# Four-layer graph network, one core: comparing a tile of ranks with itself in one operation, the diagonals of r on GpSimd, and the short tile's row sum on VectorE

## The chip, the cores and the metric

The kernel runs on 1 core of one Trainium2 chip. A core has a matrix engine (TensorE, PE in the profile; its weight loads are shown as PEld), a vector engine (VectorE, DVE), an activation engine (ScalarE, ACT), GpSimd (POOL) and a queue engine (SyncE, SP). Each engine works through its own instructions in order, and waits on semaphores for the others. SP, ACT and POOL issue transfers (DMA) between the chip's memory (HBM) and the on-chip memory (SBUF); TensorE writes to a separate accumulator memory (PSUM), which is read out by VectorE or ScalarE.

The metric is device microseconds (us) of one execution. The kernel before took 853.08 us, the median of 4 runs (850.79, 852.27, 853.89 and 853.95).

## The reference, cut to what matters

Four layers work on `x` (2708 nodes by 128 features) and on `adj` (2708 by 2708, zeros and ones with ones on the diagonal). Each starts with a layer norm and a relu and adds its result to `x`. The change lies in the last layer:

```python
XW = h @ W
s_col = XW @ a[0, :f]
s_row = XW @ a[0, f:]
Z1 = leaky_relu(s_row[:, None] + s_col[None, :], negative_slope=0.01)
den = exp(Z1)
num = A @ den
att = where(num != 0, den / num, 0)
x = x + A @ (att @ XW)
```

Below, `r` is `s_row` and `c` is `s_col`, one number per node. Since `den[i, j]` is `exp(r_i + c_j)` where the sum is positive and `exp(0.01 (r_i + c_j))` where it is not, `A @ den` can be built from sums over nodes sorted by `r`. So the kernel needs the rank of every node in `r`.

## The kernel before

The 2708 nodes lie in T = 22 tiles of 128 rows; the last holds 20 rows (`rows(t)`). They are also grouped into six blocks of 512 columns (`TILES[b]`, `E0[b]`). The scheduler of the tile framework decides the order of instructions on each engine, except where a line asks for program order. The work of layer 4 goes through these stages:

1. **Making r.** For each block b the loop that ends at L727 takes the previous layer's result, transposes it, adds it to `xs`, makes the layer norm (`bn_stats` L184, `bn_aggr` L185, `isq` L172 on VectorE; a power function for `rstd` L173 on GpSimd; `shift` L189 on VectorE; the relu L191 on ScalarE), transposes again, copies to `hT` (L705, ScalarE) and multiplies by the weights (L209). The products are copied out in groups of three tiles, c = 0, 3, ..., 21 (`hs`, L210, VectorE). Column P+1 of them is r; L712 and L713 put it into `r_of`, with nodes beyond 2708 moved far away. Each group's r is then needed along the free dimension of all partitions: VectorE multiplies the identity by r (`diag`, L717), TensorE multiplies a matrix of ones by that (L724, into the one buffer `acc4`), and ScalarE copies the result to `row_b` (L727). `diag` has two buffers.
2. **Ranks.** `row_b` now has all r along the free dimension, `r_of[:, t]` has tile t's along the partitions. For tiles in groups of three (c), four VectorE operations on 128x384 elements compare a tile with itself: `own` (L735, greater), `tie` (L736, greater or equal), `tie` times the strict triangle `before` (L737), and the maximum of both (L738); `own` and `tie` have one buffer each. For each tile t, VectorE then compares all earlier tiles with it (`bits`, L744, 128 by 128t; two buffers), ScalarE sums `bits` along the row into `rowsum` (L747, with `row_a` as a place for the copy it makes), and TensorE sums `bits` and `own` down the columns (L753, L757) into one accumulator.
3. **From ranks to tables.** L761 copies the accumulator, four transposes (L764) turn it, `below` (L766) takes the row sums off, L782 makes a second copy of r in `row_a`, and L770 to L776 give `rank`. A long row of small VectorE operations follows (from `ge`, L673), with TensorE matmuls between; it orders nodes by c as well.
4. **Sums.** `sums(t)` loads tile t of the transposed adjacency (L828, SP's queue) and adds it up with weights that depend on the rank (L835). The loads of the first tiles wait in SBUF during stages 1 and 2; the others start as buffers come free.
5. **Densities.** `densities(s0)` does the same trick of diagonal (L1088), matmul (L1095), scale (L1102, L1104), L1105 and exponential (L1106) for four slots at a time. The first three calls (s0 = 0, 4, 8; `FIRST = 3`) stand between the last `sums`, the other eight after them.
6. **Main loop.** GpSimd gathers rows of the adjacency and of the prefix sums by index (L647), and for 22 steps TensorE forms `num` (L1206), ScalarE and VectorE form the attention, and TensorE adds it up (L1150). A last product with the adjacency gives the result.

Of the kernel before, what the change touches and what calls it, by code (L numbers as in the profile page):

```python
# [8 lines left out]
F32 = mybir.dt.float32  # L9
BF16 = mybir.dt.bfloat16  # L10
# [9 lines left out]
def kernel(  # L20
# [436 lines left out]
    nc.vector.memset(ones_b, 1.0)  # L457
    before = const.tile([P, P], BF16, name="before")
    nc.vector.tensor_scalar(before, lane, part, None, ALU.is_gt)
    first = const.tile([P, P], F32, name="first")  # L460
    nc.vector.memset(first, 0.0)
    nc.vector.memset(first[0:1, :], 1.0)
# [23 lines left out]
    def rest(exact, stack3):  # L486
# [182 lines left out]
        with tc.tile_pool(name="tab", bufs=1) as tab, tc.tile_pool(name="tabs", bufs=2) as tabs:  # L669
# [17 lines left out]
            for b in range(NB):  # L687
                lo, hi = E0[b]
                n = len(TILES[b])
                ts = slice(TILES[b][0], TILES[b][-1] + 1)  # L690
                nc.scalar.activation(yT[:, lo:hi], row_b[:, lo:hi], AF.Relu, bias=tot[:, 6:7], scale=tot[:, 5:6])
                p = acc_bank(b % 2)
                turned(p, yT, TILES[b], True)
                f = len([t for t in TILES[b] if t < TF])
                nc.vector.tensor_add(
                    xs[:, ts.start : ts.start + f, :].rearrange("p t d -> p (t d)"),
                    xs[:, ts.start : ts.start + f, :].rearrange("p t d -> p (t d)"),
                    p[:, : f * P],
                )
                if f < n:  # L700
                    nc.vector.tensor_add(xs[:TAIL, TF, :], xs[:TAIL, TF, :], p[:TAIL, cols(f)])
                layernorm(b, hn)
                p = acc_bank(2 + b % 2)
                turned(p, hn, TILES[b])
                nc.scalar.copy(hT[:, spans(b)], p[:, : n * P])  # L705
                t0 = done
                while done < T and min(done + 3, T) <= ts.stop:
                    project(w3_ext, done, bank())
                    done += 3

                new = slice(t0, min(done, T))
                nc.vector.tensor_mul(r_of[:, new], r_col[:, new], valid[:, new])  # L712
                nc.vector.tensor_add(r_of[:, new], r_of[:, new], far[:, new])  # L713
                for c in range(new.start, new.stop, 3):
                    m = min(3, new.stop - c)
                    diag = tabs.tile([P, 4, P], F32, tag="diag", name="diag")
                    nc.vector.tensor_tensor(  # L717
                        diag[:, :m],
                        ident[:, None, :].to_broadcast([P, m, P]),
                        r_of[:, c : c + m, None].to_broadcast([P, m, P]),  # L720
                        ALU.mult,
                    )
                    p = acc_bank(4)
                    nc.tensor.matmul(  # L724
                        p[:, : m * P], ones, diag[:, :m].rearrange("p t q -> p (t q)"), start=True, stop=True
                    )
                    nc.scalar.copy(row_b[:, c * P : (c + m) * P], p[:, : m * P])  # L727
            nc.scalar.dma_start(xw_d.rearrange("(t p) d -> p t d", p=P), hs[:, :, :P])
            for c in range(0, T, 3):
                m = min(3, T - c)  # L730
                own = tabs.tile([P, 3, P], BF16, tag="own", name="own", bufs=1)
                tie = tabs.tile([P, 3, P], BF16, tag="tie", name="tie", bufs=1)
                mine = row_b[:, c * P : (c + m) * P].rearrange("p (t q) -> p t q", q=P)
                theirs = r_of[:, c : c + m, None].to_broadcast([P, m, P])
                nc.vector.tensor_tensor(own[:, :m], mine, theirs, ALU.is_gt)  # L735
                nc.vector.tensor_tensor(tie[:, :m], mine, theirs, ALU.is_ge)  # L736
                nc.vector.tensor_mul(tie[:, :m], tie[:, :m], before[:, None, :].to_broadcast([P, m, P]))  # L737
                nc.vector.tensor_max(own[:, :m], own[:, :m], tie[:, :m])  # L738
                for q in range(m):
                    t = c + q  # L740
                    r = rows(t)
                    if t:
                        bits = tabs.tile([P, N], BF16, tag="bits", name="bits")
                        nc.vector.tensor_scalar(  # L744
                            bits[:r, : t * P], row_b[:r, : t * P], r_of[:r, t : t + 1], None, ALU.is_gt
                        )
                        nc.scalar.activation(  # L747
                            row_a[:r, : t * P], bits[:r, : t * P], AF.Identity, accum_out=rowsum[:r, t : t + 1]
                        )
                        for k in range(NB):  # L750
                            x0, x1 = E0[k][0], min(E0[k][1], t * P)
                            if x1 > x0:
                                nc.tensor.matmul(  # L753
                                    rk[:NB, : x1 - x0], pick_b[:r, k, :], bits[:r, x0:x1], start=False, stop=False
                                )
# [328 lines left out]
            def densities(s0):  # L1084
                n = min(4, NS - s0)
                diag = tabs.tile([P, 4, P], F32, tag="diag", name="diag")
                z = dmat[:, s0 : s0 + n, :]
                nc.vector.tensor_tensor(  # L1088
                    diag[:, :n],
                    ident[:, None, :].to_broadcast([P, n, P]),  # L1090
                    c_two[:, s0 : s0 + n, None].to_broadcast([P, n, P]),
# [236 lines left out]
```

## Time and profile before

| | |
|---|---|
| median of 4 runs | 853.08 us (850.79 to 853.95) |
| time of the profiled execution | 852.42 us |
| its span, first to last instruction | 850.6 us |
| PE / DVE / ACT / POOL busy | 730.5 / 583.4 / 536.4 / 190.1 us |
| stage 1 (making r), in the span | about 382 to 410 us |
| stage 2 (ranks), in the span | about 399 to 442 us |
| stage 3 and the loads of stage 4 | 442 to 506 us |
| stage 5, the last eight calls, to the start of the main loop | 506 to 534 us |

Times in the profile are microseconds from the start of the span. A timeline line has start, duration, engine, source line, operation, output<-inputs, shapes and, in brackets, how long the engine had been idle before it and what ended that. A group line has the count, the busy time in us and the mean duration in ns, and after the bar the idle time before them. The chain of work is read from the end backwards: each piece is what released the next, or what stood before it on its engine. ("issue" in it is time with no visible cause.) One row by window has the busy time and count of PE, PEld, DVE, ACT and POOL, then TensorE's granted clock as a share of full speed, the share of the DMA engines and GB/s.

### The profile page before, as it was taken

To read this page: it belongs to the slowest core of one execution; us is meant where nothing else is said; L and a number is where in the kernel's file an instruction comes from. 1 tells how busy PE (TensorE), PEld (TensorE's weight loads), DVE (VectorE), ACT (ScalarE), POOL (GpSimd) and SP (SyncE) were. 2 spreads that over 40 slices of the span, in tenths; PEclk is the share of its full clock that TensorE was granted. 3 is DMA by queue.
4 is the path that set the end of the run, shared out by engine and by line. 5 is a ranking of instruction groups with operands and counts; after the bars stand their busy time and mean duration, and the time that the engine had idled before them with its cause. 6 is when DMAs were issued, how large, how long until landed. Compare 5 with 4: busy or idle time off the path is not lost.

```text
span 850.6 us, 9005 instructions
## 1 busy us (share of the span) xinstructions
PE 730.5 (86%) x3113; PEld 440.6 (52%) x3113; DVE 583.4 (69%) x1112; ACT 536.4 (63%) x595; POOL 190.1 (22%) x161
## 2 busy tenths in 40 slices
PE   3599999995996979978759785799999999989996
PEld 2333333342775858755226531555555555545785
DVE  5499879886834363447988967776666666655854
ACT  3889999995845574537770025687777787767000
POOL 3000000012201010002000122346666667620010
PEclk9899999997897989988679995799999999999999
DMA  9044445723997989975504985677777777785994
GB/s 336 6 145 183 173 164 186 304 80 137 358 400 267 364 341 403 418 300 200 195 0 154 399 342 212 240 290 262 267 261 280 276 270 264 281 307 227 417 428 144
DMA packets 39475, 218.63 MB, mean 257 GB/s; under 512 B 5107, under 2 KB 13998, under 8 KB 25358
## 3 DMA queue, kind: packets, MB, share of 16 engines
q1 hardware_dynamic: 27704, 150.19, 45.8%
q0 software_dynamic: 8624, 65.76, 21.3%
q10 hardware_dynamic: 3090, 1.99, 0.7%
q8 instruction: 27, 0.44, 0.2%
q14 instruction: 30, 0.25, 0.1%
HBM read 214.12 MB, written 3.79 MB: 256 GB/s over the span
## 4 chain that ended last, share of the span: by engine, by line
PE 13%; DMA 12%; DVE 10%; issue 7%; POOL 6%; ACT 4%; SPq 0%; DVEq 0%; POOLq 0%; ACTq 0%
DMA hs<-in_adj_t_dram 4%; PE bank L1206 4%; PE acc L1150 3%; DMA row_b<-pre_d,pre_i 2%; DMA yT<-pre_d,pre_i 2%; POOL hs L647 2%; PE acc L224 2%; DMA row_b<-in_adj_t_dram 2%; ACT rows L1168 2%; POOL hT L647 2%; DVE bits L744 1%; POOL yT L647 1%; DVE rows L1283 1%; POOL row_b L647 1%; PE acc L835 1%
## 5 line engine op out<-in xcount | busy, mean ns | idle before, releaser
L1206 PE MATMUL bank<-rows,d_hi 128*128 128x512 f32 (+1 forms) x264 | 106.4, 407 | 24.0 <-ACT ln L1211 12.3
L224 PE MATMUL acc<-rows,h_hi 128*128 128x512 f32 (+1 forms) x264 | 106.2, 407 | 11.0 <-ACT rows L529 6.5
L1150 PE MATMUL acc<-e,xw 128*128 128x512 f32 (+1 forms) x264 | 104.3, 545 | 0.0
L1211 ACT ACTIVATE ln<-bank,tiny 128x512 f32<-128x512 f32 x132 | 79.8, 633 | 33.1 <-PE bank L1206 33.1
L1206 PE MATMUL bank<-rows,d_lo 128*128 128x512 f32 (+1 forms) x264 | 98.5, 384 | 0.0
L224 PE MATMUL acc<-rows,h_lo 128*128 128x512 f32 (+1 forms) x264 | 98.0, 387 | 0.2 <-DVE h_lo L506 0.2
L1214 DVE TENSOR_TENSOR e<-e,ln 128x1536 f32<-128x1536 f32 (+2 forms) x66 | 69.7, 1095 | 15.3 <-ACT ln L1211 15.0
L1206 PEld LDWEIGHTS bank<-rows,d_hi 128*128 128x128 f32 x264 | 51.4, 195 | 52.7 <-ACT ln L1211 29.7
L358 DVE SCALAR_TENSOR_TENSOR tau<-tau,e_hi,a 128x1536 f32<-128x1536 f32 (+1 forms) x44 | 70.5, 1623 | 10.0 <-ACT tau L355 3.9
L1150 PEld LDWEIGHTS acc<-e,xw 128*128 128x128 f32 x264 | 48.4, 190 | 52.6 <-issue 52.6
L355 ACT ACTIVATE tau<-row_a,e_neg,e_lo 128x1536 f32<-128x1536 f32 (+1 forms) x44 | 66.0, 1510 | 3.5 <-PE bank L367 3.3
L224 PEld LDWEIGHTS acc<-rows,h_hi 128*128 128x128 f32 x264 | 52.4, 199 | 24.9 <-ACT rows L529 8.6
L367 PE MATMUL bank<-tau,ones_at 128*32 128x512 f32 (+1 forms) x264 | 51.8, 566 | 8.3 <-DVE tau L358 8.3
L224 PEld LDWEIGHTS acc<-rows,h_lo 128*128 128x128 f32 x264 | 52.4, 199 | 11.7 <-issue 1.9
L1220 ACT ACTIVATE e<-e 128x2708 f32<-128x2708 f32 x22 | 54.2, 2461 | 3.6 <-DVE e L1214 3.6
L224 PE MATMUL acc<-yT,hs 128*128 128x512 f32 x132 | 56.3, 564 | 0.0
L224 PE MATMUL acc<-row_b,hs 128*128 128x512 f32 x132 | 55.3, 557 | 0.0
L1206 PEld LDWEIGHTS bank<-rows,d_lo 128*128 128x128 f32 x264 | 51.5, 195 | 7.0
L224 PE MATMUL acc<-rows,y_hi 128*128 128x512 f32 x132 | 49.1, 379 | 4.4 <-DVE rows L1283 2.5
L224 PE MATMUL acc<-rows,y_lo 128*128 128x512 f32 x132 | 47.7, 376 | 0.0
L1189 DVE TENSOR_SCALAR xw<-xw,c_exp 128x128 f32<-128x128 f32 x22 | 6.3, 285 | 58.7 <-DMA xw<-xw_d,xw_i 58.7
L529 ACT CAST rows<-dflat 128x1536 fp32r<-128x1536 f32 (+1 forms) x26 | 34.2, 1331 | 18.9 <-DMA dflat<-in_adj_dram 10.3
(411 smaller groups left out, 1419.7 us busy)
## 6 DMA issues: line engine op xcount, KB each, us to landing
a<-in_adj_dram SPq DMA_DIRECT2D x21, 1354.0 KB
rows<-in_adj_t_dram SPq DMA_DIRECT2D x16, 1354.0 KB
dflat<-in_adj_t_dram SPq DMA_DIRECT2D x9, 768.0 KB
rows<-in_adj_t_dram SPq DMA_DIRECT2D x9, 768.0 KB
dflat<-in_adj_dram SPq DMA_DIRECT2D x9, 768.0 KB
rows<-in_adj_dram SPq DMA_DIRECT2D x9, 768.0 KB
dflat<-in_adj_t_dram SPq DMA_DIRECT2D x5, 1354.0 KB
hs<-in_adj_t_dram SPq DMA_DIRECT2D x5, 1354.0 KB
```

The lines of the kernel that those rows point to most:

```text
L224: nc.tensor.matmul(accs[b][:, : hi - lo], w, moving[:, lo - at : hi - at], start=start and i == 0, stop=stop and i == len(parts) - 1,)
L355: nc.scalar.activation(tau[:, :w], row_a[:, h0:h1], AF.Relu, bias=e_neg[:, t : t + 1], scale=e_lo[:, t : t + 1])
L358: nc.vector.scalar_tensor_tensor(tau[:, :w], tau[:, :w], e_hi[:, t : t + 1], a[:, h0:h1], ALU.add, ALU.mult)
L367: nc.tensor.matmul(den[g : g + 32, : hi - lo], ones_at[:, b // GR, :], tau[:, lo - h0 : hi - h0], start=(t == 0 and b < GR), stop=(t == T ...
L529: m = nc.vector.tensor_copy(r, a) if i % 2 and i > 4 else nc.scalar.copy(r, a)
L647: return nc.gpsimd.indirect_dma_start(out=out, out_offset=None, in_=src, in_offset=bass.IndirectOffsetOnAxis(ap=idx, axis=0),)
L1150: m = nc.tensor.matmul(accs[b][:, : hi - lo], xw, e[:, lo:hi], start=(s == 0), stop=(s == NE - 1))
L1168: m = nc.scalar.copy(r, a) if q % 2 else nc.vector.tensor_copy(r, a)
L1206: m = nc.tensor.matmul(num[:, : hi - lo], d, a[:, lo:hi], start=(i == 0), stop=(i == len(products) - 1))
L1211: nc.scalar.activation(ln[:, lo:hi], num[:, : hi - lo], AF.Ln, bias=tiny)
L1214: tc.keep_in_program_order(nc.vector.tensor_sub(e[:, beg:hi], e[:, beg:hi], ln[:, beg:hi]))
L1220: tc.keep_in_program_order(nc.scalar.activation(e, e, AF.Exp))
```

## The change

- A constant `tie_at` is made once, before the layers: minus 2 to the power of -126 in the strict triangle, zero elsewhere.
- Each tile is compared with itself by one VectorE operation on 128x128: `(row_b - r_of) > tie_at`, three of them for a group of three tiles, in place of the four operations on 128x384. `own` takes the pool's two buffers; `tie` goes.
- The diagonals of r (L717) are made by GpSimd.
- The row sum of the last tile (20 rows by 2688) is a VectorE reduction in place of the ScalarE pass.
- The diagonals of the first three calls of `densities` (s0 below 12) are made by GpSimd.

```diff
+    tie_at = const.tile([P, P], F32, name="tie_at")
+    nc.vector.tensor_scalar_mul(tie_at, before, -(2.0**-126))
...
                     diag = tabs.tile([P, 4, P], F32, tag="diag", name="diag")
-                    nc.vector.tensor_tensor(
+                    nc.gpsimd.tensor_tensor(
                         diag[:, :m],
...
-                own = tabs.tile([P, 3, P], BF16, tag="own", name="own", bufs=1)
-                tie = tabs.tile([P, 3, P], BF16, tag="tie", name="tie", bufs=1)
-                mine = row_b[:, c * P : (c + m) * P].rearrange("p (t q) -> p t q", q=P)
-                theirs = r_of[:, c : c + m, None].to_broadcast([P, m, P])
-                nc.vector.tensor_tensor(own[:, :m], mine, theirs, ALU.is_gt)
-                nc.vector.tensor_tensor(tie[:, :m], mine, theirs, ALU.is_ge)
-                nc.vector.tensor_mul(tie[:, :m], tie[:, :m], before[:, None, :].to_broadcast([P, m, P]))
-                nc.vector.tensor_max(own[:, :m], own[:, :m], tie[:, :m])
+                own = tabs.tile([P, 3, P], BF16, tag="own", name="own")
+                for q in range(m):
+                    t = c + q
+                    nc.vector.scalar_tensor_tensor(
+                        own[:, q, :], row_b[:, cols(t)], r_of[:, t : t + 1], tie_at, ALU.subtract, ALU.is_gt
+                    )
...
-                        nc.scalar.activation(
-                            row_a[:r, : t * P], bits[:r, : t * P], AF.Identity, accum_out=rowsum[:r, t : t + 1]
-                        )
+                        if t == T - 1:
+                            nc.vector.tensor_reduce(rowsum[:r, t : t + 1], bits[:r, : t * P], AX.X, ALU.add)
+                        else:
+                            nc.scalar.activation(
+                                row_a[:r, : t * P], bits[:r, : t * P], AF.Identity, accum_out=rowsum[:r, t : t + 1]
+                            )
...
                 z = dmat[:, s0 : s0 + n, :]
-                nc.vector.tensor_tensor(
+                (nc.gpsimd if s0 < 4 * FIRST else nc.vector).tensor_tensor(
                     diag[:, :n],
```

## The prediction

> **What bounds the kernel now.** I read the page, then the windows, to see which engine fills the stage that the change touches, then the chain of work there, then the timelines of VectorE and ScalarE. Everything that is edited lies in 382 to 442 us, but for three diagonals at 493 to 498 us and one constant.
>
> ```profile
> 397.00:410.00 13.00, 10.44 (x47) 6.01 (x48) 12.36 (x51) 7.25 (x22) 0.84 (x1) 0.91 0.54 180
> 410.00:442.00 32.00, 21.73 (x83) 8.15 (x82) 27.61 (x53) 29.28 (x38) 0.00 (x0) 0.71 0.22 73
> ```
>
> From 397 to 410 VectorE is full (12.36 of 13 us) and GpSimd idle. From 410 to 442 VectorE (27.61 of 32) and ScalarE (29.28) are both nearly full. The chain of waits goes through both:
>
> ```profile
> 410.42 0.20 ACT row_a L747
> ...
> 410.64 0.62 DVE bits L744
> 411.27 0.46 DVE own L735
> ...
> 438.08 2.54 ACT row_a L747 x2
> ...
> 440.65 0.18 DVE below L766
> ...
> 442.23 0.17 DVE rank L770
> ```
>
> ScalarE's timeline shows when its row sums start and where they halt:
>
> ```profile
> 408.36 0.48 ACT L727 COPY row_b<-acc 128x384 f32<-128x384 f32 x1 [3.09 <-PE acc L724]
> ...
> 413.55 1.06 ACT L747 ACTIVATE row_a<-bits 128x1024 f32<-128x1024 bf16 x1
> ...
> 416.48 1.27 ACT L747 ACTIVATE row_a<-bits 128x1280 f32<-128x1280 bf16 x1 [0.49 <-DVE bits L744]
> ...
> 421.38 1.59 ACT L747 ACTIVATE row_a<-bits 128x1664 f32<-128x1664 bf16 x1 [0.43 <-DVE bits L744]
> ...
> 433.26 2.23 ACT L747 ACTIVATE row_a<-bits 128x2432 f32<-128x2432 bf16 x1
> ```
>
> So the sums wait 3.09 us for the copies of r; later ScalarE sets the pace but for 0.92 us in which VectorE is late. I cut at two points: A, from 390.35 (the first diagonal) to the sum of tile 8 (413.55); B, from there to the sum of tile 19 (433.26); C, from there to `rank` (442.23). What follows (VectorE's table operations without a pause to 485, then loads at 0.87 to 0.99 of the DMA engines to 504, then gathers) waits for `rank` or for buffers freed after it, so a shift of `rank` should reach the end whole.
>
> **Prices.**
>
> ```profile
> L735 DVE TENSOR_TENSOR own<-row_b,r_of 128x384 bf16<-128x384 f32 x7 | 3.9, 550 | 0.5 <-PE acc L757 0.5
> ...
> L737 DVE TENSOR_TENSOR tie<-tie,before 128x384 bf16<-128x384 bf16 x7 | 2.4, 348 | 0.0
> ...
> L1105 DVE SCALAR_TENSOR_TENSOR dflat<-dflat,flatter 128x512 f32<-128x512 f32 x11 | 8.2, 747 | 3.0 <-ACT dflat L1102 3.0
> ...
> L339 DVE TENSOR_REDUCE deg<-a 128x1 f32<-128x2708 f32 x2 | 5.9, 2964 | 0.0
> ...
> masks.py:199 POOL TENSOR_SCALAR_AFFINE_SELECT ident<-ident 128x128 f32<-128x128 f32 x1 | 0.3, 293 | 0.0
> ...
> L75 POOL MEMSET hn<- 128x1172 f32 x1 | 1.7, 1704 | 35.0 <-DVE rows L529 35.0
> ...
> L75 POOL MEMSET row_b<- 128x1172 f32 x1 | 1.1, 1077 | 5.0 <-DVE rows L529 5.0
> ```
>
> - *Own comparison.* Starts of consecutive VectorE instructions lie 0.08 us closer than their durations, so four old operations hold VectorE 2 x 0.47 + 2 x 0.27 = 1.48 us per group. The new one is L1105 at 128 instead of 512 elements: two-input rows grow 1.05 ns per element (L1088's 512 against L717's 384: 682 - 542 ns), so 0.747 - 0.40 = 0.35; L735 at 128x128 took 0.29, the low end. I take 0.30 and 0.22 of VectorE's line: 0.66 per group, 0.8 saved seven times.
> - *Diagonal on GpSimd, 128x384.* No row shows a GpSimd multiply. L173 is a power function, not near. The select took 0.293 for 128 elements, one read and one write; memsets (0.205 at 128, 2.36 at 2708) give a fixed 0.1, so 1.5 ns per element for two streams, 2.25 for three: 0.1 + 384 x 2.25 ns = 0.97 us, which I take. Low end: VectorE's 0.55. High end: the memset of `hn` beside VectorE's copies took 1.58 times its twin: 1.53 us.
> - *Reduction, 20x2688 bf16.* L339 scaled: 2.94 us, taken as the nearest row. Low end: half, 1.5, since L737 on 16-bit data takes 0.35 where L735 takes 0.55.
>
> A weighing: the Trainium skill, "GPSIMD Engine Reference", section 3.1, has a two-input elementwise operation of 2048 elements at 4497 ns on GpSimd against 2293 on VectorE, and says VectorE stays the rule. My estimate from it is 0.84 us for 384 elements, by which the sum below would be 0.3 us better.
>
> **A.** I stepped the new order of each engine with the durations of these rows and of the timeline. (The old order, stepped alike, gives 413.28 for the sum of tile 8 where the trace has 413.55, so I compare stepped with stepped.) VectorE's line loses 8 diagonals (7 x 0.47 + 0.2 = 3.5 us) and, up to tile 8, 3 x 1.48 us of old comparisons; it gains 12 x 0.22 and ten small operations on `r_exp` and `r_low`, 0.8 us, that ran later: 4.5 us less. Not all of it is gain. A chain takes its place: diagonal 0.97, matmul 0.75, copy 0.48 us per group, through one PSUM buffer, with three L209 products now standing behind the first diagonal's matmul on TensorE, so the copy of group c=3 moves from 395.08 to 396.2 and that of c=15 from 404.8 to 405.7. GpSimd's queue hides only the next `rstd`, which the first diagonal ends in time for (390.85 against 392.29). The one DMA in ScalarE's queue there (`xw_d`, L728) stays at its place, 405.2 against 405.34; SP's queue is not passed. But ScalarE no longer has the copies of c=18 and 21 ahead of the sums of tiles 4 to 6: tile 4 starts at 406.1 (409.89 before). Then VectorE is late again: it does six own comparisons (1.3) and eleven small ones (1.2) before the bits of tile 6, so tile 6 comes at 409.8 (411.50) and tile 8 at 412.3. A = 412.3 - 413.3 = -1.0. With 0.55 us per diagonal it is -2.0, with 1.53 it is +1.3.
>
> **B.** ScalarE's durations for tiles 8 to 18 sum to 17.50 us, plus 11 x 0.12 between starts: 18.8, against 19.7. VectorE has slack now (bits of tiles 8 to 20 plus ten comparisons are under 16 us), and `own` no longer waits for TensorE with two buffers: -0.9. Ends: -0.9, and 0 if the halts stay.
>
> **C.** The bits of tile 21 wait for the sum of 19 (2.36 after its start), take 1.61, the reduction 2.94; then L761, which now stands behind it (0.60), `below` (0.10) and L782 (1.48): 9.06 with gaps, against 8.97. +0.1. ScalarE's pass of 2.44 goes, but something of equal length takes its place. With a reduction of 1.5 TensorE's column sums of tile 21 are next (439.69 in the trace): -0.4.
>
> **Nothing for the rest.** The constant (0.2 us) falls into VectorE's 0.54 us wait at 15 us. The three diagonals at 493 us: 128x512 by the same row is 1.25 us from 492.9; TensorE comes to the first at 495.2, behind sums that wait for loads. If that cover went, 0.6 us. The gather behind them on GpSimd's queue starts at 503, after loads; the third diagonal is over near 497.6.
>
> Sum: -1.0 - 0.9 + 0.1 = -1.8: the profiled execution's 852.42 becomes 850.6 (span 848.8). It was 0.66 under the median; on the median's scale 853.08 - 1.8 = **851.3 us**.
>
> **Does GpSimd hold up VectorE?** Two-input VectorE operations inside a GpSimd instruction ran at normal length (L712 at 399.71 in 0.15 us, inside the `rstd` of 399.50, and the pair below), though that instruction reads only four elements per partition:
>
> ```profile
> 392.36 0.15 DVE L713 TENSOR_TENSOR r_of<-r_of,far 128x3 f32<-128x3 f32 x1
> 392.29 1.01 POOL L173 TENSOR_TENSOR rstd<-isq,neg_half 128x4 f32<-128x4 f32 x1 [3.57 <-DVE r_of L712]
> ```
>
> The Trainium skill's page "SBUF — State Buffer", section "SBUF: two separate sides", says the pair of SBUF ports shared by VectorE and GpSimd is an exclusive lock, for VectorE operations with two SBUF inputs or two ports. Stepped with such a lock, tile 8 comes at 413.2 and the sum is -0.9 instead of -1.8.
>
> **Rivals.**
> 1. *GpSimd becomes the bound (slower).* One mechanism: six diagonals in a row (c=3 to 18) carry r to ScalarE, each on the chain. Above 1 us every 0.1 us per diagonal costs 0.4. The point of no gain is 1.4 us. At 2.0 us A is +3.5, the sum +2.7: 855.8. For it: 1.53 by the contended memset, and VectorE is at 12.36 of 13 us there. Against: 0.97 by the select.
> 2. *More gain.* Diagonals at 0.55, comparisons at 0.21 per operation, the short reduction: A -2.4, B -0.9, C -0.4 = -3.7: 849.4. For it: VectorE's waits for TensorE at a clock of 0.71 shrink. Against: nothing shows GpSimd level with VectorE.
> 3. *No change.* The load of `row_b` at 489.06 takes 15.03 us behind others; if the loads are held by bandwidth and not by `rank`, the shift is eaten: 853.1. Against: no byte moves from 420 to 442, so loads start only after `rank`.
>
> **Chances and range.** About 0.3% (2.6 us) is what a measurement of this kernel can tell from no change. Forecast 0.48 (its own range 849.5 to 853, four tenths of it past 0.3%), more gain 0.21, slower 0.20, no change 0.11. Faster 0.19 + 0.21 = 0.40, same 0.29 + 0.11 = 0.40, slower 0.20. The range runs from 1 us of run scatter below rival 2, 848.4, to rival 1 at 2.0 us, 855.6.
>
> **What would show it.** Right: POOL diag rows near 1 us; the sum of tile 4 near 406 and of tile 8 near 412, no halt from there; `rank` near 440.4; the reduction near 2.9 us. Wrong: POOL diag rows above 1.4 us, VectorE rows stretched beside them, or `rank` early and the loads' end at 504 not.

## The result, and the profile after

| | before | after |
|---|---|---|
| median of all runs | 853.1 us (70 runs, 847.56 to 859.31) | 853.48 us (44 runs, 849.22 to 858.91) |
| ratio after / before, 95% interval | | 1.0011 [1.0000, 1.0021] |
| profiled execution, its span | 852.42, 850.6 us | 855.91, 854.1 us |
| first r_of (L712, after: L715) | 389.44 | 390.07 |
| from there to the sum of tile 8 | 24.11 | 25.28 |
| sum of tile 8 to sum of tile 19 | 19.71 | 19.15 |
| sum of tile 19 to `rank` | 8.97 | 9.03 |
| first r_of to `rank` | 52.79 | 53.46 |
| `rank` to the landing of the load into `row_b` | 61.90 | 64.58 |

By the ratio the kernel became slower by 0.1%, 0.9 us, where 1.8 us less was forecast. (The medians of all runs lie only 0.4 us apart, and the interval begins at no change; the forecast gain lies outside it.) The stage begins 0.63 us later in the profile of after than in that of before, ahead of everything in the stage that was changed; in all the profiles below the first r_of lies anywhere from 388.96 to 391.71 us. So all stages are counted from the first r_of. (Lines of after are 3 or 4 higher than before's: L720 is the diagonal, L730 the copy to `row_b`, L737 the own comparison, L745 `bits`, L749 and L751 the row sums, L774 `rank`, L839 the sums.)

The two windows of the stage, after:

```profile
397.00:410.00 13.00, 10.28 (x48) 6.37 (x47) 8.90 (x28) 8.36 (x26) 4.93 (x7) 0.87 0.55 195
410.00:443.00 33.00, 19.27 (x84) 7.82 (x84) 28.05 (x57) 25.61 (x33) 0.34 (x1) 0.88 0.22 73
```

VectorE, which was full (12.36 of 13 us) from 397 to 410, now counts 8.90 us, and GpSimd 4.93 instead of 0.84. Yet the stage is no shorter. ScalarE's timeline shows where it halts:

```profile
407.95 0.48 ACT L730 COPY row_b<-acc 128x384 f32<-128x384 f32 x1 [1.36 <-PE acc L727]
408.33 0.63 ACT L751 ACTIVATE row_a<-bits 128x512 f32<-128x512 bf16 x1
...
413.05 0.84 ACT L751 ACTIVATE row_a<-bits 128x768 f32<-128x768 bf16 x1 [3.01 <-DVE r_exp_p L793]
...
415.35 1.06 ACT L751 ACTIVATE row_a<-bits 128x1024 f32<-128x1024 bf16 x1
```

Tile 4 does start earlier (18.26 us after the first r_of; 20.45 before), but then ScalarE waits 3.01 us for VectorE, and tile 8 is 1.17 us late. VectorE's timeline has two reasons. Rows that take longer than elsewhere show when GpSimd's timeline is laid beside it, and brackets show waits for TensorE:

```profile
391.24 0.38 DVE L172 TENSOR_SCALAR isq<-mv 128x4 f32<-128x4 f32 x1
...
394.48 0.73 DVE L172 TENSOR_SCALAR isq<-mv 128x4 f32<-128x4 f32 x1
...
399.64 2.03 DVE L737 SCALAR_TENSOR_TENSOR own<-row_b,r_of,tie_at 128x128 bf16<-128x128 f32 x3
...
405.02 0.56 DVE L210 COPY hs<-bank 128x390 f32<-128x390 f32 x1 [2.28 <-PE bank L209]
...
408.34 0.55 DVE L745 TENSOR_SCALAR bits<-row_b,r_of 128x640 bf16<-128x640 f32 x1 [0.78 <-PE acc L757]
...
408.88 2.40 DVE L737 SCALAR_TENSOR_TENSOR own<-row_b,r_of,tie_at 128x128 bf16<-128x128 f32 x6
```

```profile
390.77 0.83 POOL L720 TENSOR_TENSOR diag<-ident,r_of 128x384 f32<-128x384 f32 x1 [1.43 <-PE acc L198]
...
394.37 0.83 POOL L720 TENSOR_TENSOR diag<-ident,r_of 128x384 f32<-128x384 f32 x1 [1.66 <-DVE r_of L716]
...
399.86 1.66 POOL L720 TENSOR_TENSOR diag<-ident,r_of 128x384 f32<-128x384 f32 x2 [1.68 <-DVE r_of L716]
...
409.11 1.23 POOL L720 TENSOR_TENSOR diag<-ident,r_of 128x384 f32<-128x384 f32 x2 [2.16 <-DVE r_of L716]
```

For comparison, two of these operations on VectorE with no GpSimd multiply beside them (own_only, below):

```profile
391.55 0.16 DVE L172 TENSOR_SCALAR isq<-mv 128x4 f32<-128x4 f32 x1
...
405.53 0.86 DVE L737 SCALAR_TENSOR_TENSOR own<-row_b,r_of,tie_at 128x128 bf16<-128x128 f32 x3
```

An `isq` on four elements per partition takes 0.16 us there; the one that begins at 394.48 ends at 395.21, with the diagonal (394.37 + 0.83 = 395.20). The one at 391.24 ends at 391.62, the diagonal at 391.60. Three own comparisons that take 0.86 us undisturbed take 2.03, six take 2.40 instead of 1.72. In these four rows 0.22 + 0.57 + 1.17 + 0.68 = 2.6 us of VectorE's time count as busy and are waiting. The prices themselves, in the groups of after, are near those forecast:

```profile
L737 DVE SCALAR_TENSOR_TENSOR own<-row_b,r_of,tie_at 128x128 bf16<-128x128 f32 x22 | 8.5, 429 | 0.2 <-PE acc L761 0.2
...
L720 POOL TENSOR_TENSOR diag<-ident,r_of 128x384 f32<-128x384 f32 x7 | 5.8, 834 | 10.7 <-DVE r_of L716 5.5 <-PE acc L727 2.4 <-PE acc L198 1.4
...
L749 DVE TENSOR_REDUCE rowsum<-bits 20x1 f32<-20x2688 bf16 x1 | 2.9, 2941 | 0.0
```

The mean of 429 ns for the own comparison contains the held ones.

### The profile page after: what moved, and what is told of

Its sections match the earlier page's. It is cut to its first block, busy times and chain, and to the rows that moved or that the text cites. A ratio compares the mean times of both kernels' runs of the same rounds, so it can differ in the third digit from the quotient of the medians.

```text
span 854.1 us, 8999 instructions
## 1 busy us (share of the span) xinstructions
PE 728.6 (85%) x3113; PEld 440.8 (52%) x3113; DVE 578.5 (68%) x1093; ACT 533.6 (62%) x593; POOL 202.4 (24%) x172
## 4 chain that ended last, share of the span: by engine, by line
PE 46%; DVE 14%; DMA 13%; POOL 9%; ACT 9%; issue 9%; SPq 0%; DVEq 0%; POOLq 0%; ACTq 0%
PE acc L224 25%; PE bank L367 6%; DMA hs<-in_adj_t_dram 4%; PE bank L1210 4%; PE acc L1154 3%; DMA row_b<-in_adj_t_dram 2%; DMA row_b<-pre_d,pre_i 2%; DMA yT<-pre_d,pre_i 2%; POOL hT L650 2%; ACT row_a L751 2%; ACT rows L1172 2%; POOL rstd L173 2%; DMA rows<-in_adj_t_dram 2%; POOL hs L650 2%; PE acc L839 2%
```

## The experiments

Three theories stood against each other. **L**: a GpSimd multiply holds up the VectorE operations that begin beside it. **T**: no hold-up; what costs is the new order of instructions (so in the expectation of own_only) or the longer way to `row_b` over GpSimd and TensorE (so in those of diag_only and own_dummy). **D**: what follows `rank` (TensorE's clock, loads paced by the DMA engines) eats any shift. The readings of all profiles come first, in us, one profile a row; each is told below. The "own group" are five profiles of kernels with the one-operation own comparison, VectorE's diagonals of r and nothing added: own_only, own_again, diag_back, back_again, own_reduce. The five "with the old comparison" are before, before2, before3, dens_only and const_only.

| profile | r_of to sum of tile 8 | r_of to `rank` | `rank` to end of half speed | `rank` to landing | ratio [95%] |
|---|---|---|---|---|---|
| before | 24.11 | 52.79 | 6.30 | 61.90 | |
| before2 | 23.86 | 52.16 | 7.16 | 62.68 | 1.0002 [0.9981, 1.0023] |
| before3 | 23.57 | 51.42 | 7.23 | 61.80 | 0.9988 [0.9968, 1.0008] |
| dens_only | 24.36 | 52.30 | 6.52 | 61.89 | 1.0005 [0.9980, 1.0030] |
| const_only | 23.84 | 52.15 | 7.25 | 62.55 | 1.0002 [0.9978, 1.0026] |
| reduce_only | 23.57 | 52.52 | 6.10 | 60.38 | 1.0010 [0.9990, 1.0029] |
| diag_only | 24.46 | 52.72 | 6.04 | 61.75 | 1.0029 [1.0004, 1.0054] |
| own_only | 22.32 | 50.14 | 8.44 | 63.85 | 1.0017 [0.9993, 1.0041] |
| own_again | 23.17 | 50.99 | 7.02 | 62.62 | 0.9995 [0.9975, 1.0016] |
| diag_back | 22.32 | 50.21 | 8.38 | 64.52 | 0.9990 [0.9973, 1.0006] |
| back_again | 22.08 | 50.13 | 7.62 | 62.18 | 0.9981 [0.9955, 1.0006] |
| own_reduce | 22.32 | 50.21 | 8.69 | 63.93 | 0.9982 [0.9962, 1.0001] |
| own_dummy | 24.94 | 52.77 | 6.52 | 61.78 | one run |
| after | 25.28 | 53.46 | 8.71 | 64.58 | 1.0011 [1.0000, 1.0021] |
| after2 | 24.13 | 52.21 | 6.87 | 62.26 | 1.0036 [1.0014, 1.0058] |
| sums_11_15 | 22.32 | 52.21 | 6.77 | 62.08 | 1.0020 [0.9999, 1.0041] |
| own_late1 | 22.33 | 53.19 | 8.83 | 63.12 | 1.0025 [1.0007, 1.0043] |
| wait_2 | 22.33 | 52.35 | 6.76 | 62.34 | 1.0019 [0.9990, 1.0048] |
| warm | 23.19 | 51.09 | 6.95 | 60.67 | 0.9998 [0.9973, 1.0022] |
| late3 | 24.21 | 61.89 | 7.30 | 62.50 | 1.0096 [1.0071, 1.0121] |

The landing is read at the first matmul that uses the loaded `row_b`. "Half speed" is the stretch in which TensorE's granted clock is 0.50 around `rank`.

### The parts alone: own_only, diag_only, reduce_only, diag_back, dens_only

```diff
own_only: before, with
+    tie_at = const.tile([P, P], F32, name="tie_at")
+    nc.vector.tensor_scalar_mul(tie_at, before, -(2.0**-126))
...
-                nc.vector.tensor_tensor(own[:, :m], mine, theirs, ALU.is_gt)
...
+                    nc.vector.scalar_tensor_tensor(
+                        own[:, q, :], row_b[:, cols(t)], r_of[:, t : t + 1], tie_at, ALU.subtract, ALU.is_gt
+                    )
```

> The kernel before with the one-operation comparison alone (own, tie_at); the diagonals stay on VectorE, the last row sum on ScalarE. Theory L (GpSimd's two-input diagonals hold VectorE's two-input and two-port operations for their whole length, which cost the changed kernel about 3 us of VectorE's line in 390 to 412 us): without GpSimd the saving of 0.8 us per group shows, rank 2 to 3 us earlier against the start of the stage than before, ratio 0.996 to 0.998. Theory T (the order that the scheduler makes once the comparison is one operation is what costs, lock or no lock): rank no earlier than before, ratio 1.000 to 1.002. Theory D (what comes after rank eats any shift): rank earlier, but the ratio within 0.001 of 1.

```diff
diag_only: before, with
-                    nc.vector.tensor_tensor(
+                    nc.gpsimd.tensor_tensor(
                         diag[:, :m],
```

> The kernel before with the diagonals of r on GpSimd alone. L: VectorE rows beside POOL diag rows stretched to the end of the POOL row, rank 1 to 3 us later than before, ratio 1.001 to 1.004. T: POOL diag rows of 0.83 us on the chain and no stretched rows; rank within 1 us of before. D: ratio within 0.001 of 1 wherever rank lands.

```diff
reduce_only: before, with
+                        if t == T - 1:
+                            nc.vector.tensor_reduce(rowsum[:r, t : t + 1], bits[:r, : t * P], AX.X, ALU.add)
+                        else:
```

> The kernel before with the last tile's row sum on VectorE alone. All theories: the pass of 2.44 us on ScalarE is replaced by a reduction of 2.94 us on VectorE behind which the copy of the accumulator stands, so rank 0.1 us later counted from the start of the sum of tile 19; ratio 0.9995 to 1.0005.

```diff
diag_back: after, with
-                    nc.gpsimd.tensor_tensor(
+                    nc.vector.tensor_tensor(
                         diag[:, :m],
```

> The changed kernel with the diagonals of r back on VectorE (comparison, row sum and the three density diagonals as changed). L: no stretched VectorE rows in the ranks stage, rank 2 to 3 us earlier than before, ratio 0.996 to 0.998. T: rank as in the changed kernel, about 0.7 us later than before, ratio about 1.001. D: rank earlier, ratio within 0.001 of 1.

The own comparison alone puts `rank` at 50.14 us, where the five profiles with the old comparison have 51.42 to 52.79, mean 52.16. The own group has a mean of 50.34: 1.8 us earlier. So the order that comes with the new comparison does not cost by itself, as T had it at first. The diagonals on GpSimd alone give 52.72, although they take 3.5 us off VectorE's line. Added to the own comparison (diag_back to after and after2) they cost 2.0 to 3.3 us at `rank`. The row sum of the last tile costs nothing beside the new comparison: from the sum of tile 19 to `rank` own_only needs 8.96 us and diag_back 9.03. With the old comparison it does: reduce_only needs 10.06 us where 0.1 more than 8.97 was expected, because the last maximum for `own` (L738) stands behind the reduction there, and the copy of the accumulator (L764) comes after it and after the second copy of r (L785).

But the whole kernel does not follow `rank`: own_only's ratio is 1.0017, and L's 0.996 to 0.998 was missed by both own_only and diag_back (0.9990). diag_only is the one part whose interval leaves out no change. Its rows are stretched as L has it (`bits` on 128x256 in 0.93 us, 0.35 beside nothing), but its `rank` is only 0.6 us behind the mean, where L expected 1 to 3, so its stage does not account for the 2.5 us of its ratio.

```diff
dens_only: before, with
-                nc.vector.tensor_tensor(
+                (nc.gpsimd if s0 < 4 * FIRST else nc.vector).tensor_tensor(
                     diag[:, :n],
```

> The kernel before with the first diagonals of the densities on GpSimd alone (the part of the change not yet run alone). All theories: they lie beside the loads into row_b and hT, first r_of to `rank` as in the kernel before (52.2 to 52.8 us), ratio 1.000. If their GpSimd multiplies hold VectorE or the software queue's gathers behind them on GpSimd: up to 2 us slower.

1.0005 [0.9980, 1.0030], stage and landing as before: the diagonals of the densities cost nothing that can be told from scatter, as forecast.

### The hold-up by itself: own_dummy

```diff
 own_only, with, behind each diagonal of r on VectorE,
+                    scrap = tabs.tile([P, 3, P], F32, tag="scrap", name="scrap", bufs=1)
+                    nc.gpsimd.tensor_tensor(
+                        scrap[:, :m],
+                        ident[:, None, :].to_broadcast([P, m, P]),
+                        r_of[:, c : c + m, None].to_broadcast([P, m, P]),
+                        ALU.mult,
+                    )
```

> The kernel before with the one-operation own comparison, VectorE making the diagonals of r, and beside each diagonal one GpSimd multiply of the same size (128x384, the same operands) into a tile that nothing reads: the chain from r_of to row_b is VectorE's, as in the kernel with the own comparison alone, whose first r_of lay 50.14 us ahead of `rank`. Theory L (a GpSimd multiply holds up VectorE's operations that begin beside it): VectorE's rows beside the multiplies are stretched until they end, as in the changed kernel, and first r_of to `rank` is 52 to 54 us. Theory T (the changed kernel's loss is the longer way over GpSimd to row_b): 50.1 to 50.6 us, rows of normal length.

`rank` came at 52.77, 2.6 us behind own_only, inside L's 52 to 54 and far from T's 50.1 to 50.6. Nothing reads what these multiplies write. (One thing still stands behind them: a `rstd` in GpSimd's queue, from whose `isq` to whose `shift` it takes 1.62 us instead of 0.92; up to 0.7 of the 2.6 us may be that.) VectorE's timeline of own_dummy beside them, and then GpSimd's:

```profile
393.87 0.78 DVE L189 SCALAR_TENSOR_TENSOR shift<-mv,rstd 128x4 f32<-128x4 f32 x1 [0.72 <-POOL rstd L173]
...
402.82 0.55 DVE L720 TENSOR_TENSOR diag<-ident,r_of 128x384 f32<-128x384 f32 x1
403.29 0.85 DVE L752 TENSOR_SCALAR bits<-row_b,r_of 128x128 bf16<-128x128 f32 x1
...
408.40 1.65 DVE L744 SCALAR_TENSOR_TENSOR own<-row_b,r_of,tie_at 128x128 bf16<-128x128 f32 x3
```

```profile
393.80 0.83 POOL L727 TENSOR_TENSOR scrap<-ident,r_of 128x384 f32<-128x384 f32 x1
...
402.78 1.27 POOL L727 TENSOR_TENSOR scrap<-ident,r_of 128x384 f32<-128x384 f32 x1 [0.67 <-DVE r_of L716]
```

The four-element `shift` lasts until the multiply ends (394.65 against 394.63) instead of 0.15 us; the first `bits`, 0.28 us in own_only, takes 0.85 and ends at 404.14, the multiply at 404.05. It works both ways: the multiply that meets VectorE's own 0.55 us diagonal takes 1.27 instead of 0.83 us. So the hold-up of L is shown.

It is not shown that the hold-up is the whole loss of the changed kernel (2.0 and 3.3 us against diag_back in two profiles), since that kernel also saves the 3.5 us of diagonals that own_dummy's VectorE still makes. Its trace has a second loss, which is T's: up to the `bits` of tile 6 VectorE waits 3.4 us for TensorE in after and 2.1 in after2, 0.3 in own_only and not at all in own_dummy. On TensorE the products for `hs` (L209) stand among the matmuls that wait for GpSimd's diagonals. Hold-up and waiting are of like size, and no run separates the two in the changed kernel.

### Does a shift of `rank` reach the end? late3, before2, sums_11_15

```diff
late3: before, with
             below = tab.tile([P, T], F32, name="below")
+            for _ in range(3):
+                nc.vector.tensor_reduce(rowsum[:r, T - 1 : T], bits[:r, : t * P], AX.X, ALU.add)
```

> The kernel before with three more row sums of the last tile on VectorE ahead of `rank`, 2.94 us each in the changed kernel's profile, so that `rank` comes 8.8 us later and nothing else moves. If a shift of `rank` reaches the end whole: +8.8 us, 861 us. Theory D (what follows `rank` gives a part back: the TensorE clock is back at full speed when the first sums run, 0.7 us, and the loads behind are paced by the DMA engines): +4 to +8 us.

The delay itself is 9.0 us (from the sum of tile 19 to `rank` 17.96 us instead of 8.96); `rank` lies 9.7 us behind before2's. The kernel became 8.8 us slower (862.05 against 853.28; by the interval 6 to 10): a large delay reaches the end.

> The kernel before, unchanged, against itself: ratio 1.000, as every theory has it; the second profile shows how far the times of one program's stages scatter: first r_of to `rank` the same within 0.1 us, `rank` to the landing of the load into row_b within 2 us or more.

A miss: two profiles of one program differ by 0.6 us at `rank`, not 0.1, and before3 by 1.4: its TensorE ran at full clock where that of before had 13.65 us of half speed (407.5 to 421). So 2 us are at the limit of what one profile or 12 runs show here.

```diff
sums_11_15: diag_back, with
-                        if t == T - 1:
+                        if t in (11, 15, T - 1):
                             nc.vector.tensor_reduce(
```

> The changed kernel with the diagonals of r back on VectorE, and the row sums of tiles 11 and 15 on VectorE beside that of tile 20: VectorE idles about 0.5 us of 2 there and ScalarE is busy 1.97 of 2. ScalarE loses 1.35 and 1.75 us, VectorE takes 1.6 and 2.2 us: `rank` 2 to 3 us ahead of the 50.2 us after the first r_of, 5 us ahead of the kernel before. If a shift reaches the end whole: 847 to 848 us against 852.5. Theory D: 849.5 to 852 us.

A miss (the last tile, 20 in the expectation, is tile 21 in the kernel's count): `rank` came at 52.21, 2 us later than in diag_back, not 2 to 3 earlier. The sums of tiles 12 and 16 started 0.98 and 2.00 us late. With two buffers for `bits`, a row sum on VectorE stands in front of the next comparison, and ScalarE runs dry: VectorE's 0.5 us of idle time in every 2 was not slack that could be used in pieces of 1.6 us.

### The same again, and a delay put back: own_again, own_late1, after2

> The kernel with the own comparison alone once more, for a second profile and more times: first r_of to `rank` 50.1 us against 52.2 to 52.8 of the kernel before. Theory D (what follows `rank` eats an earlier `rank`: the first sums run at half clock, `rank` to `many` 17.3 us instead of 16.65, and the load into row_b takes 17 to 18 us instead of 15 to 15.6 from issue to landing): landing 0 to 1 us earlier than in the kernel before, measured from the first r_of; ratio 0.999 to 1.001. If the earlier `rank` reached the end: ratio 0.997, 850 us against 852.6.

```diff
own_late1: own_only, with
             below = tab.tile([P, T], F32, name="below")
+            for _ in range(1):
+                nc.vector.tensor_reduce(rowsum[:r, T - 1 : T], bits[:r, : t * P], AX.X, ALU.add)
```

> The own comparison alone, with one row sum of the last tile (2.94 us) on VectorE put ahead of `rank`, so that `rank` comes where the kernel before has it (52.8 to 53.1 us after the first r_of instead of 50.1); all that follows `rank` is in the same order on every engine. Theory D: `rank` to `many` back at 16.65 us, the load into row_b back at about 15.5 us, the landing 0.3 to 1 us behind that of the own comparison alone though `rank` is 2.9 us behind; times as the kernel before and as the own comparison alone within 1 us. If a shift of `rank` reaches the end whole: 2.9 us slower than the own comparison alone.

> The changed kernel once more, beside the others on one chip: first r_of to `rank` 53.4 us, VectorE's rows beside the GpSimd diagonals stretched as before, `rank` to `many` 17.4 us and the load into row_b 17 to 18 us by theory D, ratio 1.001 to 1.004; if these two were scatter of one execution, they come back to 16.65 and 15.5 us.

Theory D in its first form fell here: own_late1, with a late `rank`, has the late end of half speed (8.83 us) and own_again, with an early one, has not (7.02). And own_late1 is 2.4 us slower than own_again on the same chip (854.3 against 851.86), not within 1 us of it.

after2 shows that 1.2 us of the recorded profile's `rank` was that execution: 52.21, with VectorE's held rows again (2.04 and 2.40 us for three and six comparisons). The difference arises at one place. In after TensorE ran at half speed from 401.04 to 404.45 us, and VectorE's wait of 2.28 us for L209 falls there; in after2 the clock was full and the same wait is

```profile
403.65 0.56 DVE L210 COPY hs<-bank 128x390 f32<-128x390 f32 x1 [1.00 <-PE bank L209]
```

The two profiles of the changed kernel average 52.84, 0.7 us behind the kernels with the old comparison; after2 alone is level with them. Its time is not: 1.0036 [1.0014, 1.0058].

### What an early `rank` is worth: back_again, own_reduce, before3

back_again is diag_back once more, before3 the kernel before.

```diff
own_reduce: diag_back, with
-                (nc.gpsimd if s0 < 4 * FIRST else nc.vector).tensor_tensor(
+                nc.vector.tensor_tensor(
                     diag[:, :n],
```

> The changed kernel with the diagonals of r back on VectorE, once more: the only version so far with a ratio below 1 (0.999). First r_of to `rank` 50.2 to 51 us. Theory D, as it stands now (an execution whose half-clock stretch ends 8.6 us after `rank` lands the load into row_b 64 us after `rank`, one whose stretch ends 6.3 to 7.3 us after it 62.2 us): whichever of the two this execution shows, both numbers go together; ratio 0.997 to 1.0005. If the earlier `rank` reached the end whole: ratio 0.9975.

> The changed kernel with all diagonals, those of the densities too, back on VectorE: the own comparison and the last row sum on VectorE alone. All theories: first r_of to `rank` as with the diagonals of r alone put back, 50.2 to 51 us. Theory D: half-clock stretch until 8.6 us after `rank` and landing 64 us after it, or until 6.3 to 7.3 us and 62.2 us; ratio 0.998 to 1.001. If the earlier `rank` reached the end whole: 0.9975.

> The kernel before against itself once more: ratio 1.000; theory D: first r_of to `rank` 52.2 to 52.8 us, half-clock stretch until 6.3 to 7.3 us after `rank`, landing of the load into row_b 62.2 us after it. If the late ends of the half-clock stretch are chance and not tied to an early `rank`, one of them (8.6 us, 64 us) may show here too.

The five ratios of the own group average 0.9993; with about 0.0022 on either side for each, their mean is good to about 0.001 at best (0.0022 / sqrt 5; some of them share their runs of the kernel before). Had the 1.8 us arrived, it would be 0.9979. In the profiles the landing, counted from the first r_of, moved from a mean of 114.3 (five with the old comparison, 113.2 to 114.8) to 113.8 (own group, 112.3 to 114.7): 0.6 us of 1.8, with more scatter than that. So most of the gain seems to be gone by the landing.

Kernels with the new comparison say something else when they are compared with each other. sums_11_15, own_late1 and wait_2 (below) have `rank` 2.2 us behind the own group on average, and ratios of 1.0020, 1.0025 and 1.0019: 0.28% (give or take about 0.16%), or 2.4 us. By that a shift of 2 us does reach the end, and what keeps the own group from being faster than the kernel before lies outside the stage. The runs do not decide between the two readings. The chain of waits of own_reduce between `rank` and the landing:

```profile
445.24 9.06 PE acc L839 x57
...
487.99 17.21 DMA row_b<-in_adj_t_dram
505.24 2.73 PE acc L839 x24
```

### What ends the half speed: wait_2, warm

In the profiles TensorE's half speed comes in stretches of 3.41, 6.83, 10.24 and 13.65 us and longer, multiples of 3.41. The Trainium skill, "TensorE: Matmul & The Clock Gate", section 'Part 1: The HAM clock gate (the "warmup" mystery)', says that a monitor grants half or full clock by how busy TensorE was in a free-running window of 3413 ns; the lengths here agree. The first sums begin 2.8 us after `rank`, and in all profiles the stretch around `rank` ends 6.0 to 8.8 us after it. Where it ends 8.38 us or more after `rank`, the landing came 64.0 us after `rank` (five profiles), otherwise 62.2 us (13, without reduce_only and warm, whose sums stand in another order on TensorE). Counted from the first r_of, the end lies at 57.8 to 59.4 us in all but three: an earlier `rank` does not move it, and with a `rank` near 53.3 (after, own_late1) it slips to 62.

```diff
wait_2: own_reduce, with
+            idle = tab.tile([P, 1], F32, name="idle")
+            nc.vector.tensor_reduce(idle[:r], bits[:r, :1792], AX.X, ALU.add)
             nc.vector.tensor_sub(below, tile_base, rowsum)
```

> The own comparison and the last row sum on VectorE, all diagonals on VectorE (the kernel whose `rank` came 50.21 us after the first r_of, half-speed stretch ending 8.69 us after `rank`, landing of the load into row_b 63.93 us after it), with one more VectorE reduction of 20x1792 ahead of `rank`, 1.96 us by the row of 2.94 for 2688: nothing else changes its place on any engine. Theory C (TensorE's half-speed stretch ends on a grid of 3.41 us, at the first mark that lies 6.0 us or more behind `rank`, when TensorE has been full of the first sums for one such step; in 17 of 17 profiles the end lies 6.0 to 8.8 us behind `rank`): `rank` at 52.2, the stretch ends at the same mark as without the wait, 58 to 59.3 us after the first r_of, 6 to 7 us after `rank`; landing 62 us after `rank`, so 114.2 us after the first r_of as without the wait (114.14): the wait is free, ratio 0.997 to 1.000. If a shift of `rank` reaches the end whole: 1.96 us slower than without it, ratio 1.0005 or more.

```diff
warm: own_reduce, with
+            warm = acc_bank(3)
+            for _ in range(3):
+                nc.tensor.matmul(warm[:NB, :], pick_b[:r, 0, :], bits[:r, :512], start=True, stop=True)
             rk_sb = tab.tile([8, 512], F32, name="rk_sb")
...
                 nc.tensor.transpose(p[:, q * 8 : q * 8 + NB], rk_sb[:NB, cols(q)], ident[:NB, :NB])
+            for _ in range(4):
+                nc.tensor.matmul(warm[:, :256], rk_sb[:NB, :P], rk_sb[:NB, :256], start=True, stop=True)
```

> The same kernel without the wait, and with seven matmuls whose result nothing reads, which fill TensorE's pauses between its last column sum and the first sums (three of 20x512 bf16 ahead of the transposes, four of 6x256 f32 behind them, 3.4 us at half speed). Theory C: TensorE is busy from 6 us before its first sums on, so the half-speed stretch ends one step of 3.41 us earlier, 55 to 56 us after the first r_of, 5.2 us after `rank`; `rank` to `many` 16.6 us instead of 17.45, landing near 62 us after `rank`, 112.2 us after the first r_of: 2 us ahead of the kernel before, ratio 0.9965 to 0.999. If the half-speed stretch does not depend on how busy TensorE is: 17.4 and 64 us as before; if it is not what makes the landing late: the stretch ends earlier and the landing stays at 64 us.

wait_2's profile is what theory C expected: `rank` 2.1 us later than in own_reduce, half speed ending at 59.1 instead of 58.9 us after the first r_of, and the landing 0.55 us later (114.69 against 114.14). Its windows from 444 us, and then own_reduce's (`rank` at 442.29 and 441.31; the first r_of at 389.94 and 391.10):

```profile
444.00:446.00 2.00, 0.93 (x4) 0.15 (x4) 2.00 (x4) 0.00 (x0) 0.00 (x0) 0.50 0.00 0
446.00:448.00 2.00, 1.80 (x11) 0.62 (x11) 2.00 (x5) 0.00 (x0) 0.00 (x0) 0.50 0.00 0
448.00:450.00 2.00, 2.00 (x18) 0.96 (x16) 2.00 (x5) 0.00 (x0) 0.00 (x0) 0.74 0.04 8
```

```profile
444.00:446.00 2.00, 1.71 (x9) 0.47 (x9) 2.00 (x5) 0.00 (x0) 0.00 (x0) 0.50 0.00 0
446.00:448.00 2.00, 2.00 (x13) 0.75 (x12) 2.00 (x5) 0.00 (x0) 0.00 (x0) 0.50 0.03 8
448.00:450.00 2.00, 2.00 (x14) 0.82 (x12) 2.00 (x4) 0.00 (x0) 0.00 (x0) 0.50 0.00 0
```

The earlier sums of own_reduce run at half speed for longer, 13 and 14 matmuls per 2 us; wait_2 has 18 in the window in which its clock rises. Of the later landing after `rank` (63.93 against 62.34 us) the traces show one half: the first load of `rows` behind the sums is issued at 461.58 us in own_reduce and 461.75 in wait_2, 20.27 and 19.46 us after `rank`, and from 470 to 485 us the DMA engines are full in both (1.00 to 1.02 of their time), so these 0.8 us are not made up. The other half stays open.

But the times do not confirm a free wait: 1.0019 lies outside the 0.997 to 1.000 that theory C expected and in the range of its rival, and its interval [0.9990, 1.0048] contains both 1.000 and a full 2 us. And warm shows that "busy" is not enough. TensorE was busy 3.40 of 3.42 us from 440.28 to 443.70 at 0.50, one whole step of 3.41 us, yet the stretch ended at 58.0 us after the first r_of, 6.95 after `rank`, no step earlier. Most of these matmuls (439.16 to 442.91 us) used 6 rows of the array; whether that is why they did not count was not tried. As a faster version warm failed too (0.9998). Its landing, 60.67 us after `rank`, is near that of reduce_only (60.38), with which it shares the new order of sums; neither was faster in the end.

### The constant alone: const_only

> The kernel before with the constant `tie_at` made (0.2 us of VectorE at the start) and read by nothing; all four operations of the own comparison stay. Kernels with the one-operation own comparison that have `rank` 52.2 to 53.5 us after the first r_of stand at ratios 1.0011 to 1.0036 (mean of five 1.0022), kernels with the four operations and `rank` at 51.4 to 52.8 at 0.9988 to 1.0029 (mean of five 1.0007): about 0.15% seem to lie outside the stage. If it is the constant (its place in SBUF moves every later tile by 512 bytes per partition): ratio 1.001 to 1.002 here. If not (chance, or the own comparison itself): 1.000, from 0.998 to 1.001; first r_of to `rank` 51.4 to 52.8 us in both cases.

1.0002 [0.9978, 1.0026]: no sign that the constant sets kernels with the new comparison back. Whether they are set back at all, beyond chance, stays open. What else comes with the new comparison outside the stage, the second buffer of `own` and the missing `tie`, which move later tiles too, was not tried alone.

## Why the prediction was wrong

- **The step that failed is A**, by its assumption that GpSimd does not hold up VectorE. Forecast -1.0 for the way to the sum of tile 8. The two profiles of the changed kernel have 25.28 and 24.13, mean 24.7, against 23.95 for the five with the old comparison: +0.75 (+0.2 in after2; the other 1.2 us of after are its half-speed stretch). Without GpSimd's diagonals (own group, mean 22.44) it is -1.5, and the same multiplies with nothing reading them put 2.5 us back (24.94). "VectorE rows stretched beside them" was on the prediction's own list of signs of being wrong. The row that carried the assumption, `r_of` at 0.15 us inside a `rstd` of four elements, was a poor witness: that operation reads four elements per partition, the diagonal 384.
- **Where in A.** The milestones of after2, counted from the first r_of, follow the forecast up to the sum of tile 4 (16.99 us; forecast 406.1 - 389.44 = 16.7) and lose it on the way to tile 6 (21.72; 20.4). There the six own comparisons, forecast at 1.3 us of VectorE's line, take 2.3, 0.7 of it held. In after the clock had already put tile 4 at 18.26.
- **The rule against the row.** The Trainium skill, "SBUF — State Buffer", section "SBUF: two separate sides", was weighed and put aside. For the 128x384 multiplies the rows agree with it: VectorE's rows end with the multiply, and the 1.27 us multiply shows that it works in both directions. For the short `rstd` they do not (0.15 us inside 1.01). Stepped with that rule, tile 8 was put at 413.2, 23.8 us after the first r_of, near after2's 24.13; but the sum was then still -0.9, by B.
- **The price of a diagonal.** 0.97 forecast from memsets and a select, 0.83 measured; the estimate from the "GPSIMD Engine Reference", 0.84, was the better one. Rival 1, GpSimd as the bound from 1.4 us on, had the right sign, but its condition did not come. What came, between no change and 1.8 us slower, lies between rival 3 and rival 1. (The recorded range ends at 855.6, rival 1 at 2.0 us by its own sum at 855.8.)
- **The own comparison** was forecast at 0.22 us of VectorE's line and takes 0.26 undisturbed (three in 0.86). That its effect at `rank`, 1.8 us, equals the forecast sum of all parts is luck.
- **B**: -0.9 forecast, -0.56 measured between the two recorded profiles. But the halts that B removes belong partly to the recorded execution of before: most other profiles with the old comparison need 18.9 to 19.4 us there instead of 19.71 (late3 19.73), the changed kernel 19.05 to 19.15.
- **C**: +0.1 forecast, +0.06 measured; the reduction took 2.94 us as scaled.
- **"A shift of `rank` reaches the end whole"** was right for a late `rank` (8.8 of 9.0 us in late3, 2.4 of 3.0 in own_late1). For an early one it is in doubt: against the kernel before 0.6 of 1.8 us are left at the landing and the mean ratio is 0.9993, but among kernels with the new comparison 2.2 us cost 2.4. Rival 3, no change because the loads eat the shift, may describe the own comparison in part. The loss that the profiles show begins ahead of the loads: TensorE's first sums run longer at half speed, `many` (a table read back from TensorE behind the first sums) comes 17.3 to 17.5 us after `rank` in the five profiles with the late end and 16.6 to 16.9 in the others, and the loads behind these sums begin as much later. Why the landing then comes 1.8 us later after `rank`, and not 0.8, is not settled. In the changed kernel itself there was no early `rank` to pass on.
- **Nothing for the rest** held: dens_only 1.0005.

The versions without the GpSimd diagonals of r (diag_back and back_again, 0.9990 and 0.9981) and own_reduce (0.9982) have the lowest ratios that were found; each interval still includes no change, and they are the lowest of many.

## What to carry to other kernels

Work moved to GpSimd was not free for VectorE here: operations with two inputs in SBUF, and plain `tensor_scalar` operations, that ran beside a multiply of 0.83 us ended with it. Look for such rows beside the moved work, and test with a dummy of the same size that nothing reads, which separates hold-up from most of the latency. A busy share that falls (12.36 to 8.90 us) proves no gain, and neither does a shorter stage: read the next stage's chain for what would be late then. Before a sum of 1 or 2 us is forecast from one profile, the same stage in a second profile of the same program shows how much of it is that execution.

## What the runs showed of the hardware that was not expected

- A GpSimd multiply of 128x384 held a VectorE `tensor_scalar` on 128x4, with one tensor as its input, for up to 0.57 us beyond its 0.16, and `bits` on 128x128 for as long (0.85 instead of 0.28); three or six two-input operations in a row lost 1.17 and 0.68 us. An addition with one input from TensorE's accumulator (L698, 128x128 at 391.07 us in after, inside the multiply of 390.77) kept its 0.26 us.
- TensorE's clock fell to 0.50 for multiples of 3.41 us in every profile, around `rank` for 10.24 to 20.48 us, and the end of that stretch stayed 57.8 to 59.4 us after the first r_of in most profiles while `rank` moved from 50.1 to 52.8. Matmuls with 6 rows, back to back for 3.75 us (warm), did not end it.
- The way to `rank` of one program differed by up to 1.4 us between executions (52.79 and 51.42; 53.46 and 52.21), with the half-speed stretches that fell into it.
